# Half a key step of delay for a rotation's sums, copies in halves, rows loaded piece by piece, and key tiles of two whole rows

## Chip, core and metric

One core of a Trainium2 chip. The metric is the device time of one execution in microseconds (us); the runs before have a median of 3645.0 us (3638.3 to 3660.34, three runs). All data are float32. Engines are named as in the profile: PE (matmul), PEld (weight load of the matmul), DVE, ACT, POOL, and SP, which here does nothing but issue DMAs.

## What is computed

A batch of 16 images of 256 channels and 64 x 64 places goes through two residual layers, each behind a group normalisation (32 groups).

```python
# layer 0, per image: a convolution whose kernel is rotated by an angle that the image decides
pooled = gn(x).mean(places)
angles = tanh(relu(pooled @ ap_w1.T + ap_b1) @ ap_w2.T + ap_b2) * pi / 4       # 8 groups
rot    = bilinear_rotate(base_kernel, angles)                                   # 8 x 32 x 32 x 3 x 3
mod    = sigmoid(relu(pooled @ meta_w1.T + meta_b1) @ meta_w2.T + meta_b2)
x = x + grouped_conv3x3(gn(x), rot) * mod

# layer 1: linear attention over the 4096 places, 8 heads of 32, with a 5x5 depthwise convolution of the values
t = gn(x) as tokens (places x 256)
q, k, v = t @ Wq.T + bq, t @ Wkv.T + bkv                 # split
q, k = focus(relu(.) + 1e-6)                             # cubed, brought back to the old norm, row by row
out = q @ (k.T @ v) / (q @ sum(k)) + depthwise5x5(v)     # per head
x = x + out @ Wproj.T + bproj
```

The sum over keys, `k.T @ v`, runs over all places, so the order in which tiles of keys come does not matter to it. The depthwise convolution needs the values by place: they go to DRAM and come back in blocks of 8 x 4 places with their borders.

## The kernel before

The order of work on each engine is written out by hand (`tc.manual_schedule()`): each engine does its instructions in the order in which the program issues them, and DMAs go through SP's queue in that order too. Images follow each other in a software pipeline; while image b is in its attention, image b+1 is convolved, and image b+2 gets its statistics.

For each image b there are three stages:

- The key loop, `key_step(b, n, made)` for n up to 15; the first image does all 16 steps there, the others steps 3 to 15, since steps 0 to 2 are done within the attention of the image before. A step makes the keys and values of 256 places: `key_products` (two tiles of 128 places, j = 0 and 1, on PE), `key_bias` (three DVE instructions for each tile: L528, L529, L568), `squares`, `cube` and again `squares` of the step before, `ratio` and `root` (DVE L543 and L544, POOL L547) and `key_scale` (ACT L579) of the step two before. At every second step from 5 on, `values` adds two finished pairs of tiles to `k.T @ v` on PE (L592). `key_store` writes the values of the step before to the DRAM tensor `vpad`, which is ordered by column within a block of four (k), row (y), block (j). `load_blocks` brings blocks back into `vh`, two in each step from 7 to 14. Six value buffers go round.
- `between(b, more)`: the last keys, the first query products, `convolve(b + 1, 0)`, the first half of the depthwise convolution.
- `attention_step(b, p, chain)` for p = 1 to 17: queries, attention, transposes back (`turn_back`), output projection (`project`), sum and store. At the end of steps 3, 7 and 11 (`UNITS`) it starts the convolution of units 1, 2 and 3 of the next image; step 9 (`SECOND`) does the second half of the depthwise convolution.

The convolution of an image goes in four units of two chunks (16 rows of places). A unit's rows, with one row more on each side, lie in one buffer `xr` (the first image has a buffer for each unit). Four DMAs of 288 or 320 KB, one for each quarter q of the partitions, fill it (`load_rows`); it is free again when the convolution before has read it. At the image's upper and lower edge the channel's mean is put in by `load_edges`, on POOL.

`prepare(b)` makes the rotated kernels of image b. It is a generator: `key_step` calls `next(made)` in its middle (behind the first tile's `key_bias`) and at its end, and steps 15 to 17 of the attention call it once each. What stands between two `yield`s is issued in one go. From the tenth call on it alternates between `products` (POOL L285, writes `rtmp`) and `reduce` (DVE L301, sums it into `rot`), six times, with ACT copies into `wt` (`spread`, L316) later on. For images 2 to 15 the generator starts in the attention of the image two before, and the tenth call falls in the middle of step 6 of the key loop of the image before. For image 1 it starts in step 1 of image 0's key loop, and the tenth call falls at the end of step 5.

Before the change a tile of keys T holds every fourth place of a chunk of 512: column k = T mod 4 of all blocks, in eight rows. Its weight load reads 128 elements that lie four apart:

```python
lhsT=state[b]["x"][n // 2][:, t, T % BC:CH:BC]
```

Of the kernel before, what the change touches and what calls it, by code (L numbers as in the profile page):

```python
# [15 lines left out]
P = 128  # L16
C = 256
H = W = 64
N = H * W
HID = 64  # L20
NH, HD = 8, 32
CH = 512
NCH = N // CH
NT = N // P
ROWS = CH // W
# [3 lines left out]


UNITS, SECOND = {3: 1, 7: 2, 11: 3}, 9

STATS = {3: (0, 1), 5: (2,), 7: (3, 4), 9: (5, 6), 11: (7,)}
CROWS = CH + 2 * W
BR, BC = 8, 4
# [4 lines left out]
NV = 6  # L40
# [10 lines left out]
def conv_attention(ctx: ExitStack, tc: tile.TileContext, x, consts, kw, b1, w2, b2, b2r,  # L51
                   wkv, wq, brow, srow, wp, bp, dwb, band, out):
    nc = tc.nc
# [30 lines left out]
    state = {}  # L84
# [59 lines left out]
    def rows_of(b, u):  # L144
        return xbuf[u if b == 0 else 0]
# [3 lines left out]
    vbuf = []  # L149
# [40 lines left out]
    def prepare(b):  # L190

        a, pooled, mean = yield from gn_coefs(state[b]["st"], b, 0)
# [11 lines left out]
        h = sp.tile([HID, 2], F32, tag="h", name=f"h_{b}")  # L204
# [8 lines left out]
        for t in range(2):  # L213
            for j in range(4):
                nc.tensor.matmul(pmod[ts(j, HD), t, :], lhsT=h[:, 1:2].to_broadcast([HID, HD]),
                                 rhs=w2_t[:, C + HD * (4 * t + j):C + HD * (4 * t + j + 1)], start=True, stop=True,
# [12 lines left out]
        edge = wtp.tile([P, NH], F32, tag="edge", name=f"edge_{b}")  # L229
# [2 lines left out]
        nc.vector.tensor_copy(edge, pe)  # L232
        state[b]["edge"] = edge
        if b == 0:
            load_edges(0, 0)
        nc.vector.tensor_scalar(mod, mod, 0.5, 0.5, ALU.mult, ALU.add)
        yield

# [93 lines left out]
        if b == 0:  # L332
            made = {k: products(*k) for k in ((0, 0), (0, 1), (0, 2), (1, 1), (1, 2))}
            made[1, 0] = own_products(1, 0)
            for t in range(2):
                for n in range(3):
                    reduce(t, n, made[t, n])
                row_sums(t)
                nc.vector.scalar_tensor_tensor(rots[t][:, 4], sel[:, 0:HD], 1.0, rots[t][:, 4], ALU.mult, ALU.add)
                if t == 0:  # L340
                    spread(0, range(4))
            for j in range(3):
                for q in (1, 3):
                    nc.vector.tensor_copy(wt[ts(q, HD), j], rots[1][ts(j, HD)])
            spread(1, (3,))
            state[b]["late"] = shifts
            return
        for t in range(2):
            for n in range(3):
                tmp = products(t, n)  # L350
                if t == 1 and n < 2:
                    spread(0, (2 * n,))
                yield
                reduce(t, n, tmp)
                if n == 2:
                    finish(t)
                yield
                if t == 1 and n < 2:
                    spread(0, (2 * n + 1,))
        for j in range(4):  # L360
            spread(1, (j,))
            yield
        for _ in range(3):
            yield
        shifts(0)
        shifts(1)

    def load_rows(b, u):


        for q in range(4):
            i, t = 2 * u + q // 2, q % 2
            lo, hi = max(0, CH * i - W), min(N, CH * (i + 1) + W)
            d = rows_of(b, u)[ts(q, HD)]
            at = W if i == 0 else 0
            nc.sync.dma_start(d[:, :, at:at + hi - lo], x[b, ts(t, P)].rearrange("(g c) n -> c g n", g=4)[:, :, lo:hi])

    def load_edges(b, u):


        for q in range(4):
            i, t = 2 * u + q // 2, q % 2
            mean = state[b]["edge"][ts(q, HD), ts(t, 4)].unsqueeze(2).to_broadcast([HD, 4, W])
            d = rows_of(b, u)[ts(q, HD)]
            for edge, at in ((0, 0), (NCH - 1, CROWS - W)):
                if i == edge:
                    if b == 0:
                        nc.scalar.copy(d[:, :, at:at + W], mean)
                    else:
                        nc.gpsimd.tensor_copy(d[:, :, at:at + W], mean)  # L390

    def convolve(b, u):

# [48 lines left out]
    nc.gpsimd.tensor_scalar(su, se, 1.0, None, ALU.add)  # L442
    nc.scalar.activation(sa, su, AF.Ln)
    for u in range(NCH // 2):
        load_rows(0, u)
    for i in range(2):
        load_stats(1, i)
    eps_t = const("eps", [P, C])
# [3 lines left out]
    for name, src, bsrc in (("kv", wkv, brow[C:3 * C]), ("q", wq, brow[0:C])):  # L452
        n = src.shape[1]
        w = xp.tile([P, 2, n], F32, tag="x", name=f"wl{name}")
# [8 lines left out]
    vpad = [dcp.tile([BC, H + 4, NJ, C], F32, tag=f"vpad{n}", name=f"vpad{n}") for n in range(2)]  # L463
# [19 lines left out]
    for (w, br), lo in zip(wl.values(), (0, 2 * C)):  # L483
# [3 lines left out]
        n = w.shape[2]  # L487
# [61 lines left out]
    def key_products(b, n, j):  # L549

        w, _ = state[b]["kv"]
        if j == 0:
            r = rp.tile([P, 2, C], F32, tag="r0", name=f"rk_{b}_{n}", bufs=5)
            state[b]["k"][n] = focus(r, f"k_{b}_{n}")
            state[b]["k"][n]["pm"] = []
        T = 2 * n + j
        pm = bank(f"pk_{b}_{T}")
        for t in range(2):
            nc.tensor.matmul(pm, lhsT=state[b]["x"][n // 2][:, t, T % BC:CH:BC], rhs=w[:, t, :],  # L559
                             start=t == 0, stop=t == 1)  # L560
        state[b]["k"][n]["pm"].append(pm)

# [6 lines left out]

    def key_store(b, n):  # L570
        for j in range(2):
            k, y = (2 * n + j) % BC, ROWS * (n // 2) + 2
            nc.sync.dma_start(vpad[b % 2][k, y:y + ROWS].rearrange("y j n -> (y j) n"),
                              vbuf[n % NV][:, j, 0:HD, :].rearrange("p c h -> p (c h)"))

    def key_scale(b, n):
        f = state[b]["k"][n]
# [122 lines left out]
    def turn_back(b, m):  # L700

        po = bank(f"po_{b}_{m}").rearrange("p (t j n) -> p t j n", t=2, j=2)
        for j in range(2):
            for t in range(2):
                nc.tensor.transpose(po[:, t, j, :], state[b]["o"][j][:, ts(t, P)], ident)  # L705
        oT = op.tile([P, 2, 2 * P], F32, tag="oT", name=f"oT_{b}_{m}", bufs=1)
        nc.scalar.copy(oT.rearrange("p t (j n) -> p t j n", j=2), po)  # L707
        state[b]["oT"] = oT

    def project(b, m):  # L710
# [29 lines left out]
    for u in range(NCH // 2):  # L740
        convolve(0, u)
        if u == 0:
            for t in range(2):
                state[0]["late"](t)
            load_edges(0, NCH // 2 - 1)
            for i in range(2, 6):
                load_stats(1, i)
        else:
            for i in {1: (0, 1), 2: (2, 3), 3: (4, 5)}[u]:
                take_stats(1, i)  # L750
                if u == 2:
                    load_stats(1, i + 4)
        for q in range(4):
            evict(0, u, q)
            settle(0, u, q)
# [44 lines left out]
    def between(b, more):  # L800

        k, f = state[b]["k"], state[b]["f"]
        query_products(b, 0)
        if more:
            convolve(b + 1, 0)
        ratio(k[NP - 2], False)
        root(k[NP - 2])
        squares(k[NP - 1], 0)
        cube(k[NP - 1])
        key_scale(b, NP - 2)  # L810
        query_bias(b, 0)
        blocked(b, 2)
        squares(k[NP - 1], 1)
        ratio(k[NP - 1], False)
        root(k[NP - 1])
        key_scale(b, NP - 1)
        squares(f[0], 0)
        cube(f[0])
        for n in range(NP - LATE, NP - 1):
            values(b, n)  # L820
        query_products(b, 1)
        query_bias(b, 1)
        values(b, NP - 1)
        if more:
            for q in range(4):
                evict(b + 1, 0, q)
        squares(f[0], 1)
        squares(f[1], 0)
        if more and b + 2 < B:
            load_stats(b + 2, 0)  # L830
        if more:
            load_rows(b + 1, 1)
        for c in range(0, HD, 4):
            depthwise(b, 0, c)
        if more:
            for q in range(4):
                settle(b + 1, 0, q)

    def attention_step(b, p, chain):
# [73 lines left out]
        if p <= NCH:  # L913
            load_blocks(b, 2 * p + 14)
            load_blocks(b, 2 * p + 15)
        if u and u < 3:
            load_edges(b + 1, u + 1)
            load_rows(b + 1, u + 1)
        if p >= 3:
            store(b, p - 3)  # L920
        if n >= 1:
            key_store(b + 1, n - 1)
        if more and p in UNITS:
            u = UNITS[p]
            convolve(b + 1, u)
# [4 lines left out]
    with tc.manual_schedule():  # L930
        fold_load(0, "q")
        made = iter(())
        for b in range(B):
            more = b + 1 < B
            state[b]["f"], state[b]["xq"] = {}, {}
            for n in range(0 if b == 0 else LEAD, NP):
                if b == 0 and n == 0:
                    load_kernels(1)
                if b == 0 and n == 1:
                    made = prepare(1)  # L940
                key_step(b, n, made)
                if n >= 1:
                    key_store(b, n - 1)
                if b > 0 and n == LEAD:
                    fold_load(b, "q")
                if n == 5:
                    fold_scale(b, "q")
                if n == 6:
                    fold_shift(b, "q")
                if 7 <= n < 15:  # L950
                    load_blocks(b, 2 * n - 14)
                    load_blocks(b, 2 * n - 13)
                if more and n == 11:
                    load_edges(b + 1, 0)
                    load_rows(b + 1, 0)
                if NP - 3 <= n < NP - 1:
                    blocked(b, n - NP + 3)
            key_store(b, NP - 1)
# [90 lines left out]
```

## Time and profile before

| | before |
|---|---|
| median of three runs | 3645.0 us (3638.3 to 3660.34) |
| the profiled execution | 3636.04 us |
| its span, first to last instruction | 3634.3 us, mean granted TensorE clock 0.990 |
| busy: PE, PEld, DVE, ACT, POOL | 96%, 74%, 63%, 55%, 45% |
| matmuls of the keys (L559), weight loads of these | 2048 of each; 972.9 and 617.8 us busy |
| copies of results before the projection (L707) | 256, 150.0 us busy |
| DMA | 514.58 MB, mean 142 GB/s |

How to read it: a float32 matmul stands in the profile as two instructions on PE and two weight loads on PEld. PEld runs beside PE, so a weight load costs time only where it is not finished when its matmul could start. A line of a group gives line, engine, operation, output<-inputs, shapes, count, then busy time and mean, then the idle time before. A line of the list of waits says who waited for whom, with the sum in us, the number of times, and the longest. A line of the timeline begins with start and duration in us; in square brackets stand the idle time before it and what ended it. In the list of windows each line has the stretch, its length, the busy time of PE, PEld, DVE, ACT and POOL (with numbers of instructions), the granted clock, the busy share of the DMA engines, and GB/s.

### The profile page before, as it was taken

The page shows a single profiled execution, that of the slowest core. Times are in us where ns is not written, and L with a number is a line of the kernel's source. Part 1 is how long each engine was busy: PE and PEld are TensorE (multiplying, and loading weights), DVE is VectorE, ACT ScalarE, POOL GpSimd, SP SyncE. Part 2 cuts the span into 40 slices and gives each one's busy share as a digit, 9 for nine tenths or more (in the row PEclk, how much of TensorE's full clock was granted, in tenths as well). Part 3 has the DMA queues.
Part 4 walks back from the last instruction along what each step waited for, and adds up shares of the span by engine and source line. Part 5 has one row for each costly group of instructions (what it writes and reads, how often), then busy time and mean ns, then how long its engine had stood idle before and what let it go on. Part 6 is the DMA issues. An engine that isn't in the chain of part 4 may idle for free. (4 is left out here: it accounts for less than half of the span.)

```text
span 3634.3 us, 114472 instructions
## 1 busy us (share of the span) xinstructions
PE 3475.8 (96%) x46568; PEld 2684.7 (74%) x46568; DVE 2289.3 (63%) x6541; ACT 2004.0 (55%) x6499; POOL 1619.8 (45%) x1803
## 2 busy tenths in 40 slices
PE   6999999999999999999999999999999999999999
PEld 3687786877768777687776867767677686876878
DVE  6766566665656756567565675656756566565656
ACT  2654646546465564645556455564555655556565
POOL 3534445444354543445435353443534545344445
PEclk9999999999999999999999999999999999999999
DMA  7462644536345363553535545255462554525342
GB/s 209 135 175 87 176 126 153 162 104 177 108 154 175 102 182 100 152 168 112 183 97 162 150 138 167 89 159 150 137 175 84 164 151 145 172 83 155 101 145 100
DMA packets 219857, 514.58 MB, mean 142 GB/s; under 512 B 26645, under 2 KB 99863, under 8 KB 207044
## 3 DMA queue, kind: packets, MB, share of 16 engines
q1 hardware_dynamic: 219332, 507.26, 45.4%
q8 instruction: 368, 6.03, 0.7%
q14 instruction: 157, 1.29, 0.1%
HBM read 371.63 MB, written 135.53 MB: 140 GB/s over the span
## 5 line engine op out<-in xcount | busy, mean ns | idle before, releaser
L559 PE MATMUL pk<-wkv,x 128*128 128x512 f32 x2048 | 972.9, 623 | 0.0
L697 POOL TENSOR_TENSOR o<-o,fm 128x256 f32<-128x256 f32 x512 | 362.1, 728 | 991.6 <-DVE o L695 870.2
L559 PEld LDWEIGHTS pk<-wkv,x 128*128 128x128 f32 x2048 | 617.8, 311 | 229.4 <-issue 30.7
L406 PE MATMUL pc<-xr,wt 32*32 32x504 f32 (+1 forms) x17568 | 607.4, 594 | 14.4 <-ACT wt L316 12.7
L406 PEld LDWEIGHTS pc<-xr,wt 32*32 32x32 f32 x17568 | 385.8, 103 | 201.4 <-issue 72.2
L715 PE MATMUL py<-oT,wp 128*128 128x256 f32 x2048 | 505.6, 390 | 0.9 <-ACT oT L707 0.7
L654 PE MATMUL pq<-wq,xq 128*128 128x256 f32 x2048 | 487.8, 381 | 0.0
L535 ACT ACTIVATE r_k<-rk 128x256 f32<-128x256 f32 x1024 | 415.1, 406 | 107.4 <-POOL rk L538 56.3
L535 ACT ACTIVATE r_q<-rq 128x256 f32<-128x256 f32 x1024 | 413.9, 408 | 81.7 <-DVE rq L529 52.4
L419 ACT ACTIVATE x<-pc,shift 128x512 f32<-128x512 f32 x256 | 165.5, 690 | 446.3 <-PE pc L406 425.0
L579 ACT ACTIVATE rk<-rk,s_k 128x256 f32<-128x256 f32 x512 | 231.7, 499 | 322.5 <-POOL s_k L547 322.5
L715 PEld LDWEIGHTS py<-oT,wp 128*128 128x128 f32 x2048 | 369.2, 189 | 51.6 <-issue 3.6
L654 PEld LDWEIGHTS pq<-wq,xq 128*128 128x128 f32 x2048 | 369.0, 190 | 41.9 <-ACT x L419 0.2
L528 DVE TENSOR_TENSOR pq<-pq,bq 128x512 f32<-128x512 f32 x256 | 177.5, 693 | 317.8 <-PE pq L654 317.8
L707 ACT COPY oT<-po 128x512 f32<-128x512 f32 x256 | 150.0, 586 | 392.7 <-PE po L705 392.1
L547 POOL TENSOR_TENSOR s_k<-s_k,phalf 128x2 f32<-128x2 f32 x256 | 176.9, 691 | 425.3 <-DVE s_k L544 419.2
L538 POOL TENSOR_TENSOR rk<-r_k,rk 128x512 f32<-128x512 f32 x256 | 327.1, 1278 | 57.2 <-ACT r_k L535 54.9
L538 POOL TENSOR_TENSOR rq<-r_q,rq 128x512 f32<-128x512 f32 x256 | 326.6, 1276 | 29.9 <-issue 29.9
L547 POOL TENSOR_TENSOR s_q<-s_q,phalf 128x2 f32<-128x2 f32 x256 | 179.1, 700 | 347.4 <-DVE s_q L544 318.2
L528 DVE TENSOR_TENSOR pk<-pk,bkv 128x256 f32<-128x256 f32 x512 | 218.5, 427 | 132.6 <-PE pk L559 131.7
L686 PE MATMUL pn<-kvx,qT 128*128 128x132 f32 x2048 | 273.3, 276 | 0.0
L629 PE MATMUL pd<-vh,band 107*32 107x128 f32 x8192 | 243.8, 277 | 22.9 <-issue 22.6
(135 smaller groups left out, 5012.4 us busy)
## 6 DMA issues: line engine op xcount, KB each, us to landing
vh<-vpad SPq DMA_DIRECT2D x256, 384.0 KB
vh<-vpad SPq DMA_DIRECT2D x256, 360.0 KB
vpad<-v SPq DMA_DIRECT2D x512, 128.0 KB
out<-x SPq DMA_DIRECT2D x128, 512.0 KB
xr<-in_x SPq DMA_DIRECT2D x182, 320.0 KB
xs<-in_x SPq DMA_DIRECT2D x224, 256.0 KB
xr<-in_x SPq DMA_DIRECT2D x62, 288.0 KB
xs<-in_x SPq DMA_DIRECT2D x16, 512.0 KB
```

The source lines that it names most:

```text
L406: nc.tensor.matmul(pcs[q].rearrange("p (r w) -> p r w", w=W)[ts(j, HD), :, to:to + n], lhsT=wt[ts(q, HD), j, k, :], rhs=g[ts(q, HD), j, r: ...
L528: nc.vector.tensor_add(pm, pm, bias)
L535: nc.scalar.activation(f["r2"][:, j, :], f["r"][:, j, :], AF.Square, accum_out=f["s"][:, k, j:j + 1])
L538: nc.gpsimd.tensor_mul(f["r"], f["r2"], f["r"])
L547: nc.gpsimd.tensor_tensor(f["s"][:, 3, :], f["s"][:, 2, :], phalf, ALU.pow)
L559: nc.tensor.matmul(pm, lhsT=state[b]["x"][n // 2][:, t, T % BC:CH:BC], rhs=w[:, t, :], start=t == 0, stop=t == 1)
L579: nc.scalar.mul(f["r"][:, j, :], f["r"][:, j, :], f["s"][:, 3, j:j + 1])
L629: nc.tensor.matmul(pd[ts(j, HD), k, :].rearrange("p (R m h) -> p R m h", R=4, m=4), lhsT=band_t[:, c + k, :], rhs=vb[:, :, :, j, c + k, :] ...
L654: nc.tensor.matmul(pq[:, j, :], lhsT=xq[:, t, ts(j, P)], rhs=w[:, t, :], start=t == 0, stop=t == 1)
L686: nc.tensor.matmul(pn[:, :, 4 * hh:4 * hh + 4], lhsT=qT[:, hh, j, :], rhs=kvx[:, hh], start=True, stop=True)
L697: nc.gpsimd.tensor_add(o, o, fm[:, 2 * (m % NCH) + j, :])
L715: nc.tensor.matmul(py[:, co].rearrange("p y (J c) -> p J y c", c=BC), lhsT=wp_t[:, t, ts(co, P)], rhs=oT[:, t, :].rearrange("p (J y c) -> ...
```

## The change

Four edits; the lines below are the core of the diff.

The rotation: one `yield` more before the products, one less before `shifts`. From the products to the last `spread`, everything is issued one call of `next` later.

```diff
             state[b]["late"] = shifts
             return
+        yield
         for t in range(2):
             for n in range(3):
                 tmp = products(t, n)
...
-        for _ in range(3):
+        for _ in range(2):
             yield
         shifts(0)
```

Rows piece by piece: `load_rows` and the former `load_edges` (now `load_edge`) take one quarter q. The first image's calls loop over q.

```diff
+PIECES = {1: ((1, 0), (1, 1)), 2: ((1, 2), (1, 3)), 4: ((2, 0),), 5: ((2, 1), (2, 2)), 6: ((2, 3),),
+          8: ((3, 0),), 9: ((3, 1), (3, 2)), 10: ((3, 3),)}
...
 def between(b, more):
...
-        if more:
-            load_rows(b + 1, 1)
         for c in range(0, HD, 4):
             depthwise(b, 0, c)
...
 def attention_step(b, p, chain):
...
-        if u and u < 3:
-            load_edges(b + 1, u + 1)
-            load_rows(b + 1, u + 1)
         if p >= 3:
             store(b, p - 3)
         if n >= 1:
             key_store(b + 1, n - 1)
+        for u, q in PIECES.get(p, ()) if more else ():
+            load_edge(b + 1, u, q)
+            load_rows(b + 1, u, q)
...
 the key loop:
-                if more and n == 11:
-                    load_edges(b + 1, 0)
-                    load_rows(b + 1, 0)
+                if more and 11 <= n < 15:
+                    load_edge(b + 1, 0, n - 11)
+                    load_rows(b + 1, 0, n - 11)
```

Tiles of keys: a tile is now two whole rows of 64 places, and its values go to `vpad` by two DMAs, one for each row.

```diff
-            nc.tensor.matmul(pm, lhsT=state[b]["x"][n // 2][:, t, T % BC:CH:BC], rhs=w[:, t, :],
+            nc.tensor.matmul(pm, lhsT=state[b]["x"][n // 2][:, t, ts(T % 4, P)], rhs=w[:, t, :],
...
 def key_store(b, n):
         for j in range(2):
-            k, y = (2 * n + j) % BC, ROWS * (n // 2) + 2
-            nc.sync.dma_start(vpad[b % 2][k, y:y + ROWS].rearrange("y j n -> (y j) n"),
-                              vbuf[n % NV][:, j, 0:HD, :].rearrange("p c h -> p (c h)"))
+            for r in range(2):
+                y = 4 * n + 2 * j + r + 2
+                nc.sync.dma_start(vpad[b % 2][:, y].rearrange("k j n -> j k n"),
+                                  vbuf[n % NV][ts(r, W), j, 0:HD, :].rearrange("p c h -> p (c h)"))
```

Copies in halves, in `turn_back`:

```diff
-        nc.scalar.copy(oT.rearrange("p t (j n) -> p t j n", j=2), po)
+        for t in range(2):
+            nc.scalar.copy(oT[:, t, :].rearrange("p (j n) -> p j n", j=2), po[:, t])
```

More of the change, by code (lines that the diff above doesn't have):

```diff
@@ L234, in prepare @@
         if b == 0:
-            load_edges(0, 0)
+            for q in range(2):
+                load_edge(0, 0, q)
         nc.vector.tensor_scalar(mod, mod, 0.5, 0.5, ALU.mult, ALU.add)
@@ L366, in prepare, with load_rows, load_edge @@
         shifts(1)
[L368 to L390, printed above, removed]
+    def load_rows(b, u, q):
+        i, t = 2 * u + q // 2, q % 2
+        lo, hi = max(0, CH * i - W), min(N, CH * (i + 1) + W)
+        at = W if i == 0 else 0
+        nc.sync.dma_start(rows_of(b, u)[ts(q, HD), :, at:at + hi - lo],
+                          x[b, ts(t, P)].rearrange("(g c) n -> c g n", g=4)[:, :, lo:hi])
+    def load_edge(b, u, q):
+        i, t = 2 * u + q // 2, q % 2
+        if i not in (0, NCH - 1):
+            return
+        at = CROWS - W if i else 0
+        to = rows_of(b, u)[ts(q, HD), :, at:at + W]
+        mean = state[b]["edge"][ts(q, HD), ts(t, 4)].unsqueeze(2).to_broadcast([HD, 4, W])
+        if b == 0:
+            nc.scalar.copy(to, mean)
+        else:
+            nc.gpsimd.tensor_copy(to, mean)
     def convolve(b, u):
@@ L444, in conv_attention @@
     for u in range(NCH // 2):
-        load_rows(0, u)
+        for q in range(4):
+            load_rows(0, u, q)
     for i in range(2):
@@ L744, in conv_attention @@
                 state[0]["late"](t)
-            load_edges(0, NCH // 2 - 1)
+            for q in range(2, 4):
+                load_edge(0, NCH // 2 - 1, q)
             for i in range(2, 6):
```

## The prediction

> **What bounds the kernel now.** I read the page first, then the list of waits, then the windows of the key loop for several batches, then the timeline there. The page:
>
> ```profile
> span 3634.3 us, 114472 instructions
> PE 3475.8 (96%) x46568; PEld 2684.7 (74%) x46568; DVE 2289.3 (63%) x6541; ACT 2004.0 (55%) x6499; POOL 1619.8 (45%) x1803
> ```
>
> PE is busy 96% of the span, every other compute engine under two thirds. So time is gained only where PE waits, where its clock is halved, or where one of its instructions gets shorter. The profiled execution took 3636.04 us (span 3634.3); the three runs have a median of 3645.0, nine above it. I work out differences on the profiled execution and take them off the median. A change below 1% (36 us) is about what the runs, 3638 to 3660 without any change, cannot tell from none.
>
> Who makes PE wait? The list of waits (us in total, times, longest):
>
> ```profile
> DVE rot L301 <- POOL rtmp L285: 140.4, 84, 1.7
> ...
> PEld pkv L592 <- ACT rk L579: 106.3, 91, 3.4
> ...
> PE pkv L592 <- ACT rk L579: 65.3, 37, 3.2
> ```
>
> PE's largest wait by far is in `values` (L592), for keys that ACT scales (L579). The first line tells where it comes from: DVE waits 84 times for the rotation's products. There are 15 rotations in the key loops (batches 0 to 14 prepare the next one) with six sums each, that is 90; 84 is 14 batches. One batch doesn't wait. Three windows, each from the first key product of step 6 to the first query product, for batches 0, 7 and 15 (columns: length, busy time of PE, PEld, DVE, ACT, POOL, clock, DMA share, GB/s):
>
> ```profile
> 125.69:169.48 43.79, 43.79 (x458) 30.86 (x453) 37.36 (x99) 35.05 (x122) 32.74 (x31) 1.00 0.68 211
> 1688.93:1739.34 50.41, 45.25 (x457) 31.10 (x452) 33.32 (x95) 31.04 (x110) 30.52 (x29) 0.97 0.62 197
> 3480.76:3523.24 42.48, 42.48 (x410) 30.13 (x405) 26.96 (x84) 27.95 (x105) 19.32 (x20) 1.00 0.62 206
> ```
>
> Batch 15 has no rotation and takes 42.48; batch 0 has one and takes 43.79; batch 7 takes 50.41 with the same work. By the starts of the same instructions in the timeline, batches 1 to 14 lie between 50.17 and 50.70, mean 50.36: 6.57 us more than batch 0. The timeline of batch 7, DVE, POOL and PE:
>
> ```profile
> 1713.60 1.05 DVE L301 TENSOR_REDUCE rot<-rtmp 128x96 f32<-128x864 f32 x1 [1.68 <-POOL rtmp L285]
> 1714.57 0.15 DVE L543 RECIPROCAL s_k<-s_k 128x2 f32<-128x2 f32 x1
> ...
> 1711.64 1.93 POOL L285 TENSOR_TENSOR rtmp<-mix,kw 128x864 f32<-128x864 f32 x1
> 1714.99 0.69 POOL L547 TENSOR_TENSOR s_k<-s_k,phalf 128x2 f32<-128x2 f32 x1 [1.43 <-DVE s_k L544]
> 1715.65 1.28 POOL L538 TENSOR_TENSOR rk<-r_k,rk 128x512 f32<-128x512 f32 x1
> 1716.89 1.91 POOL L285 TENSOR_TENSOR rtmp<-mix,kw 128x864 f32<-128x864 f32 x1
> ...
> 1728.12 0.86 PE L592 MATMUL pkv<-v,rk 128*32 128x33 f32 x32 [3.20 <-ACT rk L579]
> ```
>
> This is a ring: ratio (DVE L543, L544) 0.4, root (POOL L547) 0.7, cube 1.3, products 1.9, sum (DVE) 1.05, then the next step's ratio behind the sum: about 5.2 us a step (1711.64 to 1716.89 is 5.25). PE needs (163.60 - 125.69)/9 = 4.21 a step, by batch 0's key starts. So for six steps the scaled keys fall a microsecond a step behind, and PE waits for them. In batch 0 the products come at the end of a step and the sum in the middle of the next, because `prepare` starts in the middle of a step there and not at a query step:
>
> ```profile
> 140.56 1.93 POOL L285 TENSOR_TENSOR rtmp<-mix,kw 128x864 f32<-128x864 f32 x1
> ...
> 143.55 1.04 DVE L301 TENSOR_REDUCE rot<-rtmp 128x96 f32<-128x864 f32 x1
> ```
>
> The products have been done since 142.49 when the sum starts; the ring is open.
>
> **The change, part by part.**
>
> 1. Rotation (the `yield` before the products, one less at the end). Instructions and their number stay; from the products on each stands half a step later. In batches 1 to 14 the sum now stands between the step's two key biases, as in batch 0: its 1.05 us delays the second bias, not the ratio. DVE has cover: batch 0 is busy 37.36 of 43.79. Gain 14 x 6.57. In batch 0 the same `yield` moves the products to the middle of a step, where the others had them: it loses what they win. Net 13 x 6.57 = 85 us. Bounds: 0, if another ring takes its place, and 14 x (50.36 - 42.48) = 110. I take 85, since batch 0 is the very order.
>
> Part of the 6.57 is a halved clock: a window of batch 7, 1728.40 to 1731.80, shows PEclk 0.51, and 14 such windows of 3.4 us follow the waits, 1.7 us lost in each. [...]
>
> 2. Key tiles of two whole rows. The weight load of a key product no longer takes every fourth element. The view of the tiles gives it now, and the nearest row with neighbouring elements:
>
> ```profile
> L559 PEld LDWEIGHTS pk<-wkv,x x2048: 307/308/338, 98.6 to 3521.2; 128*128 128x128 f32 x187
> ...
> L654 PEld LDWEIGHTS pq<-wq,xq x2048: 186/190/192, 169.5 to 3613.6; 128*128 128x128 f32 x187
> ```
>
> 308 to 190 ns, but nearly always hidden: the starts of key matmuls lie 429 ns apart. Only behind short matmuls is the second one of a group late: by the starts in the trace, about 135 groups by 202 to 227 ns and 45 by some 110. For pq, behind short ones, it is 100 (eight take 1.99 instead of 1.89 us). So 135 x 0.11 + 45 x 0.11 = 20 us. Bounds 0 and 33 (all of the lateness).
>
> The price: `key_store` issues four transfers of 64 KB a step instead of two of 128: 512 more on SP. Now one takes 0.32 us to issue (0.37 with what lies between). A key step would hold 4 x 0.37 + 2 x 0.82 (`load_blocks`) + 0.43 (a row piece) = 3.6 of 4.21 us: hidden by PE. The new pattern isn't in the trace: nearest are this store, 0.32, and the three-part store of the output, 0.39; farthest 0.77 (vh) and the store's own longest, 1.03. Up to 0.49 nothing is late. I take 0.32 to 0.39, cost 0. Queued behind these issues on SP are vh blocks and row pieces.
>
> [...] The trace shows six vh blocks issued within 4.83 us, the last long before the packets of the first ones end: issues don't wait for each other's landing. [...]
>
> 3. Rows in pieces. Unit 0's four loads go from step 11 to steps 11 to 14, behind the vh blocks; unit 1's move from ahead of the depthwise stage to steps 1 and 2, behind four vh blocks (two edge copies on POOL, 0.42 each, move with unit 0's and two with unit 3's; POOL is free there). SP loses a wait ahead of the depthwise stage that hid nothing. The margins get thin. Unit 0: the convolution starts 7.1 us after step 14 (1734.2 to 1741.3 in batch 7); the last piece needs 0.4 to issue, 2.4 from issue to its first packet and 1.7 of packets: 2.6 left. Unit 1: vh packets start at 1764.8; four blocks at 1.6 us and four pieces at 1.9, one after another, end at 1778.8; sharing the engines better, about 1776.5. The convolution starts at 1778.02. Units 2 and 3 have a whole step. Bounds: 0 and 3 us for each of 30 convolutions, 90. I take a third of a microsecond, 10 us, as the estimates straddle the need.
>
> 4. Copies in halves. One ACT copy of 0.586 becomes two of 128x256; such pairs (L646) start 0.31 apart and take 0.40: 0.71. 256 x 0.13 = 33 us on ACT, covered: PE waits for oT only once, 0.7 us. First half 0.28 earlier at the very end: 0. Bounds -1 and 33.
>
> Sum: 3645 - 85 - 20 + 10 = 3550.
>
> **The rivals.**
>
> - Half relief: ACT or POOL leave part of the lag, say 3 us a batch. For: POOL is busy 32.74 of 43.79 in batch 0, and ACT 35. Against: batch 0 has no such PE wait. 3550 + 13 x 3.3 = 3593.
> - The ring stays and the change doesn't do what it says. Against: the order of instructions. 3550 + 85 = 3635.
> - Rows come late at units 0 and 1 by 2 us each: 15 x (4 + 1.7 of halved clock) = 85, less the 10 taken: 3625. For: the margins above.
> - Slower: SP becomes the bound in the key loop. With 0.77 an issue a step takes 4 x 0.82 + 2.07 = 5.35 us, 1.14 over; after eight steps 9.1 late, 6.5 past the margin, with 1.7 of clock 8.2 x 15 = 123: 3673. With 1.03: 2.18 x 8 - 2.6 + 1.7 = 16.5, x 15 = 248: 3798. It eats the whole gain from 0.71 an issue. Against: nothing from SBUF takes that long as a rule.
>
> **How the numbers follow.** Forecast 0.55, its own range 3515 (rows free, all lateness of the loads gone, batches nearer to 15's) to 3580; half relief 0.14; rows late 0.15; ring stays 0.08; slower 0.08. The range takes in half relief and half of the late rows: 3515 to 3612. Faster by over 1% (below 3609): forecast, half relief and part of the late rows, 0.80; within 1% 0.12; slower 0.08.
>
> **What would show it.** Right: no wait of rot for rtmp but six, in batch 0; PE's wait for L579 below 10 us; pk's load at 190 ns; windows of batches 1 to 14 near 43; half-clock windows nearly gone. Wrong: SP issuing stores at over 0.5 us; PE waiting at the first products of units 0 and 1; or the lag in batch 7 unchanged.

## The result, and the profile after

The changed kernel takes 3685.03 us (median of four runs, 3678.88 to 3695.22) against 3650.68 for the kernel before on the same chip: a ratio of 1.0102, with a 95% interval of 1.0082 to 1.0123. The forecast, 3550 us with a range of 3515 to 3612, was wrong, and on the wrong side. The profiled execution has a span of 3678.3 us, 44.0 longer than before, and a granted clock of 0.977 (before 0.990).

The page after:

```profile
span 3678.3 us, 115511 instructions
PE 3472.7 (94%) x46568; PEld 2410.9 (66%) x46568; DVE 2323.0 (63%) x6541; ACT 2019.2 (55%) x6755; POOL 1622.4 (44%) x1803
```

PE is as busy as before in the sum, so the 44 us are time in which it stands. The list of waits (us in total, times, longest) says for whom:

```profile
PE pc L410 <- DMA xr<-in_x: 121.8, 56, 6.4
...
DVE rot L305 <- POOL rtmp L289: 9.9, 6, 1.7
...
PE pkv L598 <- ACT rk L585: 4.8, 3, 2.7
```

The two waits that the forecast was built on have gone as forecast: `rot` for `rtmp` has only its six, in batch 0, and PE's wait for scaled keys fell from 65.3 us to 4.8. In their place stands a wait that the list before did not have: the convolution (`pc`) waits 56 times for its rows (`xr`).

The windows of the key loop, for batches 0, 7 and 15 (length, then busy time of PE, PEld, DVE, ACT, POOL, clock, DMA share, GB/s):

```profile
123.31:171.55 48.24, 43.81 (x459) 21.57 (x452) 32.93 (x90) 31.82 (x110) 31.03 (x30) 1.00 0.59 187
1715.88:1758.91 43.03, 42.83 (x458) 21.45 (x452) 36.55 (x99) 32.37 (x114) 30.86 (x30) 1.00 0.64 194
3526.55:3568.40 41.85, 41.85 (x411) 20.70 (x404) 26.98 (x84) 27.75 (x105) 19.31 (x20) 1.00 0.62 205
```

Batch 7 fell from 50.41 to 43.03; batch 0, which now has the products in the middle of a step and with them the closed ring, rose from 43.79 to 48.24. Three groups of the page (operation, shapes, count, busy time and mean ns, then idle time before them):

```profile
L410 PE MATMUL pc<-xr,wt 32*32 32x504 f32 (+1 forms) x17568 | 691.3, 647 | 140.5 <-DMA xr<-in_x 121.8
...
L564 PEld LDWEIGHTS pk<-wkv,x 128*128 128x128 f32 x2048 | 374.4, 190 | 402.7 <-issue 385.7
L722 PE MATMUL py<-oT,wp 128*128 128x256 f32 x2048 | 484.0, 379 | 0.5 <-ACT oT L714 0.5
```

The weight load of the keys is at 190 ns, as forecast. The output projection (`py`) got shorter, from 505.6 us busy and 390 ns to 484.0 and 379, which was not forecast. The convolution rose from 607.4 to 691.3 us busy (part of it runs at half clock after a wait: in batch 7 the granted clock is 0.75 from 1767.15 to 1775.53, behind the wait for unit 0's rows) and from next to no idle time to 140.5.

To see where 44 us come from, add up for each pair of neighbouring PE matmuls the time from start to start, and take the same sum of before. By group: convolution +209, `pkv` -71, `pk` -46, depthwise (`pd`) -36, `py` -22, the rest +10. The gains make 175 us, the convolution takes 209.

Two stretches of SP's timeline in batch 7 (start, duration, line), first around unit 0:

```profile
1749.39 0.34 SPq L379 DMA_DIRECT2D xr<-in_x  x1
1750.12 2.47 SPq L579 DMA_DIRECT2D vpad<-v  x4
1752.63 2.40 SPq L620 DMA_DIRECT2D vh<-vpad  x2
1755.78 0.33 SPq L379 DMA_DIRECT2D xr<-in_x  x1
1756.37 2.46 SPq L579 DMA_DIRECT2D vpad<-v  x4
1758.89 1.64 SPq L620 DMA_DIRECT2D vh<-vpad  x2
1760.63 0.98 SPq L379 DMA_DIRECT2D xr<-in_x  x1
...
1827.26 1.02 SPq L100 DMA_DIRECT2D xs<-in_x  x2
1828.33 1.59 SPq L620 DMA_DIRECT2D vh<-vpad  x2
1830.03 0.44 SPq L740 DMA_DIRECT2D out<-x  x1
1830.57 0.41 SPq L379 DMA_DIRECT2D xr<-in_x  x1
```

and PE's at the first products of the same units 0 and 2:

```profile
1760.84 1.72 PE L410 MATMUL pc<-xr,wt 32*32 32x512 f32 x24
1767.15 8.38 PE L410 MATMUL pc<-xr,wt 32*32 32x512 f32 x198 [4.60 <-DMA xr<-in_x]
...
1836.70 1.19 PE L410 MATMUL pc<-xr,wt 32*32 32x512 f32 x24
1840.53 4.40 PE L410 MATMUL pc<-xr,wt 32*32 32x512 f32 x65 [2.65 <-DMA xr<-in_x]
```

Unit 0's last piece is issued at 1760.63, two tenths before its convolution starts at 1760.84; PE goes on at 1767.15. The store's row says what fills SP (least, median and longest ns of an issue):

```profile
L579 SPq DMA_DIRECT2D vpad<-v x1024: 517/585/1779, 101.9 to 3570.1; - x171
```

A store of one row takes 0.585 us to issue, where the store before took 0.321.

The half clock: half the length of all half-clock stretches together is 85.8 us after, 37.4 before.

### The profile page after: what moved, and what is told of

Same layout as the page of the kernel before. It is cut to its first block, busy times and chain, and to the rows that moved or that the text cites. A ratio compares the mean times of both kernels' runs of the same rounds, so it can differ in the third digit from the quotient of the medians.

```text
span 3678.3 us, 115511 instructions
## 1 busy us (share of the span) xinstructions
PE 3472.7 (94%) x46568; PEld 2410.9 (66%) x46568; DVE 2323.0 (63%) x6541; ACT 2019.2 (55%) x6755; POOL 1622.4 (44%) x1803
## 3 DMA queue, kind: packets, MB, share of 16 engines
q8 instruction: 368, 6.03, 0.7%
## 5 line engine op out<-in xcount | busy, mean ns | idle before, releaser
L564 PE MATMUL pk<-wkv,x 128*128 128x512 f32 x2048 | 927.1, 599 | 0.0
L410 PE MATMUL pc<-xr,wt 32*32 32x504 f32 (+1 forms) x17568 | 691.3, 647 | 140.5 <-DMA xr<-in_x 121.8
L564 PEld LDWEIGHTS pk<-wkv,x 128*128 128x128 f32 x2048 | 374.4, 190 | 402.7 <-issue 385.7
L722 PE MATMUL py<-oT,wp 128*128 128x256 f32 x2048 | 484.0, 379 | 0.5 <-ACT oT L714 0.5
L714 ACT COPY oT<-po 128x256 f32<-128x256 f32 x512 | 165.6, 375 | 387.3 <-PE po L711 386.7
L109 DVE BATCH_NORM_STATS2 st<-xs 128x6 f32<-128x512 f32 x256 | 165.9, 685 | 237.4 <-DMA xs<-in_x 236.8
```

The costliest lines, as they stand in the source:

```text
L109: nc.vector.bn_stats(state[b]["st"][:, t, i, :], xt[:, t, :])
L410: nc.tensor.matmul(pcs[q].rearrange("p (r w) -> p r w", w=W)[ts(j, HD), :, to:to + n], lhsT=wt[ts(q, HD), j, k, :], rhs=g[ts(q, HD), j, r: ...
L564: nc.tensor.matmul(pm, lhsT=state[b]["x"][n // 2][:, t, ts(T % 4, P)], rhs=w[:, t, :], start=t == 0, stop=t == 1)
L722: nc.tensor.matmul(py[:, co].rearrange("p y (J c) -> p J y c", c=BC), lhsT=wp_t[:, t, ts(co, P)], rhs=oT[:, t, :].rearrange("p (J y c) -> ...
```

## The experiments

The measure used below, beside the time, is the length of a convolution unit: from its first matmul to its last, on the average of the 15 images that are convolved in the loop. An undisturbed unit takes 9.1 us. Before the change units 0 to 3 take 9.67, 9.09, 9.11 and 9.34 us; after it 16.35, 13.09, 12.37 and 9.42. Times 15 images, the first three units make 6.68 + 4.00 + 3.26 = 13.94, times 15, 209 us. Every ratio is to the kernel before on the same chip, with its 95% interval.

### One part alone, and all but one

**Rotation alone**, the kernel before with

```diff
+        yield
         for t in range(2):
...
-        for _ in range(3):
+        for _ in range(2):
             yield
```

> The kernel before with the rotation's half step alone. Theory P (the pieces of rows are the whole loss, the other parts gain as predicted): 13 x 6.57 = 85 us less, some 3566 us; the window from step 6 to the first query product near 44 us in batches 1 to 14 and near 50 in batch 0. Theory S (the long stores on SP are the loss) expects the same here, since neither stores nor pieces are in it. If the gain is missing, the rotation itself is at fault.

Measured: 3554.73 us, ratio 0.9741 (0.9710 to 0.9772), so 95 us less, with 83 to 106 by the interval. Its waits:

```profile
DVE rot L301 <- POOL rtmp L285: 10.0, 6, 1.7
...
PE pkv L593 <- ACT rk L580: 4.8, 3, 3.2
```

The ring is open, and this part did what it was to do.

**Keys alone**, the kernel before with

```diff
-  lhsT=state[b]["x"][n // 2][:, t, T % BC:CH:BC]
+  lhsT=state[b]["x"][n // 2][:, t, ts(T % 4, P)]
...
+  for r in range(2):
+      y = 4 * n + 2 * j + r + 2
+      nc.sync.dma_start(vpad[b % 2][:, y].rearrange("k j n -> j k n"),
+                        vbuf[n % NV][ts(r, W), j, 0:HD, :].rearrange("p c h -> p (c h)"))
```

> The kernel before with the key tiles of two rows alone: four stores a step of 0.585 us, rows loaded as before. Theory P: the 20 us of the shorter weight load are won and the stores lie hidden, some 3631 us. Theory S: SP, with 4 x 0.64 + 2 x 0.84 = 4.2 us a step before any row load, holds up the rows of unit 0, PE waits for xr there, and the time is above 3651.

Measured: 3647.49 us, ratio 0.9987 (0.9971 to 1.0003): no change that can be told. That is neither theory's time. In the profiled executions, counted from start to start, the key products are 21 us shorter in sum, but other groups give it back: `pd` 8, `pkv` 7, the queries' bias (`pbq`) 6 and `pc` 6. The 7 of `pkv` fit a closed ring, in which the keys are not what PE waits for last; for the rest no run shows the cause.

**Copies alone**, the kernel before with

```diff
-        nc.scalar.copy(oT.rearrange("p t (j n) -> p t j n", j=2), po)
+        for t in range(2):
+            nc.scalar.copy(oT[:, t, :].rearrange("p (j n) -> p j n", j=2), po[:, t])
```

> The kernel before with the copies in halves alone. All theories: within measurement of before (3655 us, plus or minus 5); ACT busy some 16 to 33 us more, PE waits as before. If it is faster or slower by over 10 us, the copies have a part in the result that I have not seen.

Measured: 3632.72 us, ratio 0.9958 (0.9943 to 0.9973), 10 to 21 us less. The forecast of 0 for this edit fell. With one copy the projection's first weight load starts 51 ns behind the copy's end and 11 ns ahead of its matmul, in median before the change; with halves, in the changed kernel, it starts 111 ns ahead, while the second half is still being copied. With one copy, in some 220 of 256 groups the first two projection matmuls started 311 ns apart and not 215. With halves only one such group is left. 220 x 0.096 = 21 us, which is what the group lost on PE:

```profile
L716 PE MATMUL py<-oT,wp 128*128 128x256 f32 x2048 | 484.0, 379 | 0.5 <-ACT oT L708 0.5
```

**Pieces alone**, the kernel before with `load_rows` and `load_edge` by quarters, `PIECES`, and the calls of the change:

```diff
-        if more:
-            load_rows(b + 1, 1)
...
-        if u and u < 3:
-            load_edges(b + 1, u + 1)
-            load_rows(b + 1, u + 1)
...
+        for u, q in PIECES.get(p, ()) if more else ():
+            load_edge(b + 1, u, q)
+            load_rows(b + 1, u, q)
...
-                if more and n == 11:
-                    load_edges(b + 1, 0)
-                    load_rows(b + 1, 0)
+                if more and 11 <= n < 15:
+                    load_edge(b + 1, 0, n - 11)
+                    load_rows(b + 1, 0, n - 11)
```

> The kernel before with the rows in pieces alone (old stores, old rotation). Theory P: the pieces are late by their own place, as in the changed kernel: units 0, 1 and 2 lengthen each image by up to 6.6 + 3.8 + 3.3 us, so 3750 to 3850 us. Theory S: with stores of 0.32 us the pieces are in time, 3651 to 3670. Between them, units 1 and 2 late alone (no stores stand near them): 15 x 7.1 = 107, some 3757.

Measured: 3717.31 us, ratio 1.0181 (1.0139 to 1.0224). The time lies between those of the two theories. Units take 11.54, 14.22, 10.57 and 9.91 us. Here the stores have their old form (0.32 us an issue), so the pieces do harm without the longer stores.

**All but the pieces**, the changed kernel with the diff just shown taken back: unit 0's rows whole at step 11, unit 1's ahead of the depthwise stage, units 2 and 3's behind the start of the unit before:

```diff
-        for u, q in PIECES.get(p, ()) if more else ():
-            load_edge(b + 1, u, q)
-            load_rows(b + 1, u, q)
...
+        if u and u < 3:
+            load_edges(b + 1, u + 1)
+            load_rows(b + 1, u + 1)
```

> The changed kernel with the rows loaded as before (rotation, key tiles and copies stay). Theory P: 3651 - 85 - 20 = some 3545 us, PE waits for xr under 10 us in all. Theory S: PE still waits for unit 0's rows behind the stores, above 3600.

Measured: 3540.19 us, ratio 0.9701 (0.9670 to 0.9731); units 9.84, 9.11, 9.24 and 9.36. So the whole loss belongs to the pieces: 3540 without, 3685 with them, and 145 us against the 63 that they cost alone. In the profiled executions that is 202 us more for the convolution and 52 less for the depthwise stage. Part of it is clock: half the length of the half-clock stretches is 85.8 us with the pieces and 16.5 without. With the other parts in, the same piece has less time: unit 0's last piece is issued 6.1 us ahead of its convolution with the pieces alone, and 0.4 in the changed kernel, on average. Some of that is the longer stores (next section); that the rest is the shorter steps of the key loop is argued, not run by itself.

### Is it SP's issue time, or the place of the pieces?

**One store for each key tile**, the changed kernel with

```diff
-            for r in range(2):
-                y = 4 * n + 2 * j + r + 2
-                nc.sync.dma_start(vpad[b % 2][:, y].rearrange("k j n -> j k n"), ...)
+            y = 4 * n + 2 * j + 2
+            nc.sync.dma_start(vpad[b % 2][:, y:y + 2].rearrange("k r j n -> (r j) k n"), ...)
```

> The changed kernel with one store for each key tile (both rows in one DMA of 32x4x256) instead of two: 512 issues less on SP. Theory Q (in unit 0 it is SP's queue, filled by four stores of 0.585 us a step, that holds up the pieces): if a store of the double size takes about as long to issue, SP needs some 3.5 us a step, unit 0's convolutions fall from 16.4 us towards 11 to 12 (as with the old stores), units 1 and 2 stay, and the time falls by some 15 x 5 = 75 us to about 3610. Theory R (it is the place of the pieces behind the vh blocks and the load of the DMA engines, whatever the stores): unit 0 stays above 15 and the time above 3660.

Measured: 3671.48 us, ratio 1.0073 (1.0051 to 1.0094). A store of two rows takes 0.552 us to issue, so SP's stores cost half, but unit 0 only falls from 16.35 to 15.18, as theory R had it; unit 2 falls from 12.37 to 10.85, and unit 1 rises from 13.09 to 14.37. Unit 0's last piece is now issued 3.6 us ahead of the convolution, on average, instead of 0.4, and that is still too late. The number of stores is a small part of it.

**Earlier pieces for units 1 and 2**, the changed kernel with

```diff
-PIECES = {1: ((1, 0), (1, 1)), 2: ((1, 2), (1, 3)), 4: ((2, 0),), 5: ((2, 1), (2, 2)), 6: ((2, 3),),
+PIECES = {1: ((1, 0), (1, 1), (1, 2), (1, 3)), 4: ((2, 0),), 5: ((2, 1), (2, 2), (2, 3)),
```

> The changed kernel with unit 1's four pieces all at step 1 (behind two vh blocks and not four) and unit 2's last piece at step 5, ahead of that step's loads of the statistics, and not at step 6 behind them. Theory Q: units 1 and 2 are late by what stands ahead of them in SP's queue. Unit 2 falls from 12.4 to 9.1 to 9.5 us (its last piece no longer waits for the statistics' buffer), unit 1 from 13.1 to 10 to 11; unit 0 stays at 16; the time falls by 15 x 5 = 75 us to about 3610. Theory R (the DMA engines are too busy there, the queue's order does not matter): both units stay within a microsecond of the changed kernel's and so does the time, 3670 to 3690.

Measured: 3604.52 us, ratio 0.9893 (0.9869 to 0.9917). Units 1 and 2 fell to 9.34 and 10.15; unit 0, not touched, stayed at 16.78. That is near theory Q, in the time and in the units. The last piece is now issued 11.4 us (unit 1) and 17.1 us (unit 2) ahead of its convolution, where it was 9.6 and 6.1. The place decides, unit by unit, and the lead alone does not tell what is enough. In the changed kernel 8.8 us were enough for unit 3 (9.42 us), whose last pieces come after the last blocks, and 9.6 were not for unit 1 (13.09 us), whose pieces stand among six blocks; no run changes the blocks there and keeps the lead.

**All pieces in time**, the kernel just told with unit 0 moved too:

```diff
-                if more and 11 <= n < 15:
-                    load_edge(b + 1, 0, n - 11)
-                    load_rows(b + 1, 0, n - 11)
+                if more and 8 <= n < 12:
+                    load_edge(b + 1, 0, n - 8)
+                    load_rows(b + 1, 0, n - 8)
```

> The kernel after, with unit 0's pieces at steps 8 to 11 of the key loop instead of 11 to 14, unit 1's four at attention step 1, unit 2's last at step 5. Theory Q (rows in pieces cost nothing once the last piece is issued some 12 us or more before its convolution): convolution units of 9.1 to 9.9 us, PE waiting for xr less than 10 us in all, time within 15 us of the kernel with whole loads (3540): 3535 to 3555. Theory R (the pieces themselves, or the loads they meet, cost): unit 0 stays above 12 us and the time above 3580.

Measured: 3506.97 us, ratio 0.9626 (0.9592 to 0.9660). Units 9.63, 9.51, 10.58 and 9.45. Unit 0's last piece is issued 13.6 us ahead in the image shown, and PE's wait for `xr` is down from 121.8 us to 1.1:

```profile
1449.14 0.44 SPq L379 DMA_DIRECT2D xr<-in_x  x1
...
1462.75 10.13 PE L410 MATMUL pc<-xr,wt 32*32 32x512 f32 x288
```

```profile
PE pm L171 <- DVE mv L165: 19.3, 2, 16.1
PE pc L410 <- issue: 19.2, 14, 2.4
...
PE pc L410 <- DMA xr<-in_x: 1.1, 1, 1.1
```

Only places in the order were moved, and some 175 us are gone (1.0102 to 0.9626 of 3650). But the theory had 3535 to 3555: pieces in time are better than whole loads, by 0.9701 against 0.9626, some 27 us. By the sums from start to start that is the depthwise stage, at 48 us less than with whole loads, and the convolution, at 23 more.

### What the pieces won: PE's own instructions

With whole loads (the kernel of all but the pieces) PE stands in the depthwise stage, and the profile names no releaser. Its list of PE's waits, and the timeline in one image (the line number of the depthwise matmul differs a little from kernel to kernel):

```profile
PE pd L631 <- issue: 34.8, 27, 3.3
```

```profile
1491.84 2.17 PE L631 MATMUL pd<-vh,band 107*32 107x128 f32 x71
1496.64 1.67 PE L631 MATMUL pd<-vh,band 107*32 107x128 f32 x36 [2.64 <-issue]
```

The same place with pieces in time has no gap:

```profile
1476.43 3.81 PE L635 MATMUL pd<-vh,band 107*32 107x128 f32 x132
```

What PE waits for there is read from the DMA part of the page, which has a queue of instructions:

```profile
q8 instruction: 368, 6.03, 0.7%
```

That is 368 packets, in the trace 16,384 bytes each. 46,568 matmuls and as many weight loads make 93,136 instructions; 6.03 MB over these is 65 bytes each; that the packets are PE's is read from this number. A packet then holds about 126 matmuls with their loads (before the change, 256 of PE's and PEld's instructions start between the ends of two packets, in median), and the depthwise stage, at 28 ns from start to start where nothing waits, uses one up in 3.6 us. In the stretch shown, one packet ended at 1487.16 and the next ran from 1493.87 to 1495.24; between them stand the packets of unit 1's whole load, issued from 1487.63 on (1489.04 to 1496.63). PE went on 1.40 us after the packet. Of 28 waits of over 0.5 us between depthwise matmuls in that kernel, all 28 end 1.0 to 1.7 us after the end of such a packet; before the change 19 of 19 (27.8 us in all), each 1.25 to 1.64 us after. Of all depthwise matmuls there only 12% start 1.0 to 1.7 us behind one.

Two runs test this. **Unit 1's load moved**, in the kernel before:

```diff
 def between(b, more):
-        if more:
-            load_rows(b + 1, 1)
         for c in range(0, HD, 4):
             depthwise(b, 0, c)
 def attention_step(b, p, chain):
             key_store(b + 1, n - 1)
+        if more and p == 1:
+            load_rows(b + 1, 1)
```

> The kernel before with one line moved: unit 1's whole load (four DMAs) goes from ahead of the depthwise stage to the end of attention step 1. Theory F (PE's own instructions, fetched by the same DMA engines in packets of 16 KB, come late behind that load, and PE stands in the depthwise stage for it): the waits inside runs of depthwise matmuls, 27.8 us in 19 places before, fall below 5 us, unit 1 stays at 9.1 to 9.8 us a unit, and the time falls by 25 to 40 us, to 3605 to 3620. Theory A (these waits are for ACT's copies out of the depthwise banks, which the load does not touch): the waits stay above 20 us and the time within 8 us of the kernel before.

Measured: 3631.02 us, ratio 0.9954 (0.9927 to 0.9981), 7 to 27 us less. The list has

```profile
PE pd L629 <- issue: 9.3, 12, 2.2
```

where it had 22.6 us in 19 waits before. By starts, the waits inside the depthwise stage fell from 27.8 us in 19 places to 12.1 in 11. ACT's copies did not move, so that theory falls. But 11 waits stay, all 11 behind an instruction packet, and the convolution took 21 us more, with 14 waits behind such a packet (21.5 us) where it had 9 (7.7 us): much of the stall has only moved to where the load is now. In the two profiled executions, 3635.32 and 3636.04 us, the two stages cancel, 22 less and 21 more, so where the 7 to 27 us of the medians come from they do not show. Theory F had the place right and the size too high.

**The best combination of whole loads**: rows as before, copies in halves, one store for each tile of keys, and the rotation's `yield` for images 2 to 15 only (`if b > 1:`), since image 1's rotation loses by it. To the kernel of all but the pieces this is

```diff
-        yield
+        if b > 1:
+            yield
...
-        for _ in range(2):
+        for _ in range(2 if b > 1 else 3):
             yield
...
-            for r in range(2):
-                y = 4 * n + 2 * j + r + 2
-                nc.sync.dma_start(vpad[b % 2][:, y].rearrange("k j n -> j k n"), ...)
+            y = 4 * n + 2 * j + 2
+            nc.sync.dma_start(vpad[b % 2][:, y:y + 2].rearrange("k r j n -> (r j) k n"), ...)
```

> Rows as before, copies in halves, key tiles of two rows with one store each, and the rotation's half step for images 2 to 15 alone (image 1's rotation, in image 0's key loop, keeps its old order). Against the kernel without pieces (3540 us): image 0's key loop wins the 6.6 us back, some 3533 us; if the stores of 0.585 us cost anything there, a few us more. Were it slower than 3540, the good order of image 0 would not be what made its key loop short.

Measured: 3522.51 us, ratio 0.9654 (0.9623 to 0.9684), some 10 us faster than expected; what the store and what the order of image 0 bring was not run apart. With **unit 1's load moved** as above:

> The best combination with whole loads (rows as before, copies in halves, one store of both rows of a key tile, the rotation's delay for images 2 to 15), and unit 1's load moved as in the kernel beside it. Theory F: the waits inside depthwise matmuls, 43.9 us in 26 places without the move, fall below 5 us, and the time goes from 3522 to 3470 to 3490. Theory A: 3515 to 3530.

Measured: 3500.16 us, ratio 0.9604 (0.9576 to 0.9633). The waits inside the depthwise stage fell from 43.9 us in 26 places to 11.0 in 10, as in the other pair. The convolution took 12 us more here, and the profiled execution is 32 us shorter, the median 22. The time lies between those of the two theories, and the intervals of the two kernels just overlap. **With pieces in time** in place of whole loads, that is, the same diff made to the kernel with all pieces in time:

> As the kernel before this one, with one store of both rows of a key tile and the rotation's delay for images 2 to 15 only (the best combination so far, 3522, but with pieces in time instead of whole loads). Theory Q: pieces and whole loads are alike when both are in time: 3515 to 3535. Theory R: above 3560.

Measured: 3507.52 us, ratio 0.9620 (0.9592 to 0.9648), below theory Q's 3515 to 3535, and no better than without this diff (0.9626). With pieces in time the stall behind instruction packets is in the convolution: the kernel with all pieces in time has 19 such waits there (30.7 us), the one of all but the pieces 11 (11.4 us), which is most of the 23 us above. The last three intervals overlap. The fastest median, 3500 us, has rows loaded whole; once the rows are in time, pieces and whole loads can't be told apart.

## Why the prediction was wrong

**Part 1, rotation: right.** 85 us were forecast; alone it gives 95, interval 83 to 106. Image 0's loss was forecast too (43.79 to 48.24 in its window). The half clock: the trace's reading of 14 stretches of 1.7 us was 24 us; alone, this part takes 18 of the 37.4 us away.

**Part 2, keys: the shorter load right, its worth and its price not.** From the rows 20 us were forecast for the shorter weight load. `pk` falls by 21 with the rotation alone and by 46 with all parts, so the term itself measured 25. In the time it is not to be seen, neither alone nor with the ring open: rotation alone and copies alone give 0.9741 x 0.9958 = 0.9700, and with the keys too (all but the pieces) it is 0.9701; the intervals leave some 17 us either way. In the profiled executions other groups give it back there too, `pbq` 6 and `pc` 4 of them. The step "I take 0.32 to 0.39, cost 0" failed by its number: 0.585. The nearest row was a store of another pattern. The forecast said that "up to 0.49 nothing is late". Four stores with what lies between took 2.47 us and two blocks 1.64 (timeline above), and with a piece that is 4.6 or more, in a step of PE of 4.1 (1720.72 to 1753.49 for eight steps). Still, halving the stores gave back only 11 us by the ratios (1.0102 to 1.0073), out of 145. One reading beside this sum was off: of the six vh blocks the last was issued at 1767.33, after the first block's packets had ended (1766.73). That issues don't wait for a landing stands, since three were issued by 1765.68, before any packet had ended (1765.75).

**Part 3, rows in pieces: this is the step that failed.** "I take a third of a microsecond, 10 us": it was 209 on the convolution, and 145 in the time. Three things were wrong in the margin of 2.6 us for unit 0.

- The issue. The forecast let the last piece be issued at the end of step 14. SP doesn't stand there: it has four stores and two blocks ahead of the piece, and stores wait for values (27.5 us in 40 waits for `v`, over the whole run). In batch 7 step 15 starts on PE at 1753.49 and the piece is issued at 1760.63, 7.1 us later; the convolution starts 7.35 after step 15. Even with half the stores the piece was 3.7 us behind (1740.95 to 1744.67).
- The way. 4.5 us from issue to the last packet were taken, 0.4 + 2.4 + 1.7. It was 5.8 (1760.63 to 1766.46), and 6.5 to PE's next matmul: the packets came along with some 0.7 MB of blocks and 0.4 MB of stores between 1760.6 and 1767. In unit 1 the four pieces of batch 7 were issued from 1790.17 on, and their packets ran from 1791.65 to 1805.28, past the start of the convolution at 1802.99: 13.6 us for the pieces, mixed with the packets of six blocks issued from 1788.40 on. From the first packet of a block (1789.99) it was 15.3 us to the pieces' last; the estimate had 14.0 for four blocks and the pieces one after another, and 11.7 if they share better, and there were 13.0 to the convolution.
- Unit 2: "Units 2 and 3 have a whole step". In SP's queue the statistics' loads stand ahead of unit 2's last piece. In batch 7 they waited 8.3 us for DVE (`st`), until 1827.24, and the piece was issued at 1830.57, 6.1 us before its convolution. The text named the queue behind the stores, but not this one. Unit 2 cost 49 us, and unit 1 60.

A sentence of this part was wrong in the other direction: that SP only loses there "a wait ahead of the depthwise stage that hid nothing". With the load at that place PE stood until an instruction packet had come: moved alone, it took the waits inside the depthwise stage from 27.8 us to 12.1, and after the change `pd` is 36 us shorter. The wait was in the list before: `pd` for `issue`, 22.6 us in 19 waits.

**Part 4, copies: 0 forecast, 10 to 21 us measured.** The wait that PE shows for `oT` was one of 0.7 us, but the price was paid in the weight load, which started 11 ns ahead of its matmul and, with halves, 111.

Without the pieces the forecast's sum is 3645 - 85 - 20 = 3540; the kernel without them took 3540.19. That the two agree is luck: the rotation gave 95 and not 85, the copies 15 and not 0, and the keys' 20 are not to be seen.

**The rivals.** "Rows come late at units 0 and 1 by 2 us each" named the right wait and two of its three places, and less than half its size, 85 us: units 0 and 1 came 6.7 and 4.0 us late, half clock included, and unit 2 3.3, 209 us in all. "SP becomes the bound" had the place of unit 0 and a time that takes in the measured one (3673 to 3798), but decided from 0.71 us an issue; before the change the stores took 0.321 (`vpad`) and 0.394 us (`out`) in median, the new ones take 0.585, and the runs show that stores alone are not it. That its time fits is luck. The two are one mechanism: a deadline at the end of a full queue. Taken apart, each looked small. The signs listed as wrong, "SP issuing stores at over 0.5 us" and "PE waiting at the first products of units 0 and 1", both came true.

## What to carry to other kernels

A load with a deadline is to be timed from where its queue really stands, by the last issue in the trace, and by the time to its last packet beside the transfers that share the engines there: here 6 to 14 us from issue to use, where the sum had 4.5. The change's moves of loads closer to their use lost time, and the more the faster the rest was: 63 us on the kernel before, 145 with the other parts in. A wait of PE that the list puts down to `issue`, in a stage of very short matmuls (here 28 ns from start to start), is worth a look at the instruction packets, and at which big load was issued just before.

## What the runs showed of the hardware

- Instructions come by DMA: the page has 368 packets of 16,384 bytes on a queue of their own, 0.7% of the time of the 16 engines, or one for some 126 matmuls with their weight loads (PE's by their number); in the depthwise stage they are 3.9 us apart in median before the change. All 19 waits inside that stage ended 1.25 to 1.64 us after the end of a packet, which had started 4.0 to 12.8 us after the one before it. What decides how late a packet comes behind a load was not tried; nor is it settled why 11 such waits stay after the load has moved.
- In these three stores the time to issue did not go by the size: 0.321 us for 128 KB with one row of 1 KB to a partition, 0.585 for half of that with the 64 partitions split in 16 x 4, and 0.552 for 128 KB split in 32 x 4.
- The granted clock fell to half behind waits of PE of some 2 to 3 us, and not behind all of them: after the change, counted from start to start, 9 of the 11 waits of 2.25 to 3.25 us were followed within 3 us by a half-clock stretch, and 2 of the 16 of 1.25 to 1.75; before the change, 8 of the 14 waits of 1.9 us in the key loops of batches 1 to 14 were.
